# A mixture of experts computed by sorted blocks of 256 rows instead of all tokens, in a two-layer state-space kernel

## The chip, the cores and the metric

One Trainium2 chip, one NeuronCore. The metric is the device time of one execution in microseconds (us); the lower the better. The core has a matrix engine (PE), a vector engine (DVE), a scalar engine (ACT), GpSimd (POOL) and a sync engine (SP) whose only work here is to issue DMAs. [...] engines wait for each other by semaphores.

## The reference

Four images of 384 channels and 32 x 32 positions (1024 tokens each), all in fp32, pass two layers. Each layer adds a "mixing" branch and then a feed-forward branch.

- Layer 0 mixing: four selective scans per image (rows, columns, and both reversed), then a layernorm. Layer 0 feed-forward: a small factored one.
- Layer 1 mixing: a Mamba block with 768 inner channels (input projection, a convolution of four taps, selective scan, gate, output projection, layernorm).
- Layer 1 feed-forward: a mixture of four experts. Gate scores are softmaxed, the two largest of four are kept and rescaled to sum 1, and each expert is a 384 -> 1536 -> 384 network with GELU. The result for a token is the sum of its two experts' outputs, weighted by the gates.

The parts that matter:

```python
dt = softplus(dt @ dt_proj_w.T + dt_proj_b)
# for t in tokens:
dA    = exp(dt_t * A)
h_new = dA * h_prev + dt_t * B_t * x_t        # 16 states per channel
y_t   = sum(h_new * C_t)
# experts, for each token:
out = sum over the two chosen e of gate_e * (gelu(x @ w1[e] + b1[e]) @ w2[e] + b2[e])
```

## The kernel before, in words

**Units and passes.** The work is cut in half-images of 512 tokens, called units `(b, h)`: image `b`, half `h`. The selective scans of both layers make 48 passes of three parts, and each part has four steps, so there are 576 steps in all. A step handles 32 channels times 16 states as four 128 x 512 tiles.

**One step.** POOL multiplies `dt*u` by B (`times_b`, line 1184, one instruction of 128 x 2048). ACT makes four decays `exp(dt*A)` in PSUM (`decay`, line 1190). DVE scans four times (`scan`, line 1199). The product with C is shared: DVE does two to four of the quarters (`times_c`, line 1230), POOL the rest (`times_c_pool`, line 1241). PE adds the states up with four small matmuls (`add`, line 1219) into the PSUM bank `acc`. The products of four consecutive steps lie in a ring of four tiles `s`.

**The order.** No scheduler works at run time. The kernel's Python contains a planner (`Plan`). It holds a cost for each instruction, keeps a planned clock for each engine, and emits instructions in the order in which that plan would start them. The step's instructions are "main" streams. Everything else (layernorms, projections, convolutions, the experts) runs as "lanes" that are fitted into the gaps, by rank. The experts have the lowest rank, so during the scans they only fill PE's gaps. When the last step is over, a job called `tail` hands the scan's buffers and its five PSUM banks to the other lanes.

**dt.** For each pass, `prep_pass` (lines 453 to 459) makes dt of three tiles: three small matmuls, bias by ACT, one `Softplus` on 128 x 1536 with its activation table loaded before it and the exp/ln table loaded again after it, then three products by POOL.

**Experts.** `front` (line 835 on) loads a finished unit of layer 1 from DRAM, normalizes it into `tb`, and works out the gates `sc`, which are zero for the two experts not chosen. `experts` runs all four experts on all 512 tokens of the unit: `first` multiplies by w1 (line 971, three matmuls of 512 columns for each of 12 hidden tiles), ACT adds the bias (line 974), `gelus` applies GELU with a table load on both sides (line 989), `second` multiplies by w2 (line 1026). `add_up` multiplies the result by the gate on DVE (lines 1055 and 1057) and adds it up on POOL (line 1060). Weights stream from DRAM in tiles of 192 KB (lines 925 and 932), 96 of them for a unit. Nearly all are issued from ACT's queue, in pieces of 512 bytes.

Of the kernel before, what the change touches and what calls it, by code (L numbers as in the profile page):

```python
# [10 lines left out]
F32 = mybir.dt.float32  # L11
AF = mybir.ActivationFunctionType
# [5 lines left out]
P = 128  # L18
# [15 lines left out]
NE = 4  # L34
QROW = 32
# [4 lines left out]
for _name, _w in (  # L40
    ("dtb0", 4 * NC),
    ("dtb1", NI),
    ("ds0", 4 * NC),
    ("d1", NI),
    ("lnw0", NC),
    ("lnb0", NC),
    ("lng1", NC),
    ("lnb1", NC),
    ("convw", NI * 4),
    ("convb", NI),  # L50
    ("kron1", NC),
    ("b1", NE * NF),
    ("b2", NE * NC),
):
    _PV[_name] = (_n, _w)
    _n += _w
# [192 lines left out]
def layers(ctx, tc, ins, out, const):  # L249
# [41 lines left out]
    tmp = Free(tiles(5, [P, NC, T], "tmp"))  # L291
# [3 lines left out]
    tbs = Free(tiles(1, [P, NC, T], "tb"))  # L295
    yas = Free(tiles(1, [P, NC, T], "ya"))
    mw1 = Free(tiles(3, [P, NC, P], "mwa"))
    mw2 = Free(tiles(3, [P, NC, P], "mwb"))
    NK = T // P
    scs = tiles(2, [P, NK, NE], "sc")  # L300
# [52 lines left out]
    x2 = {(b, h): dram.tile([D, T], F32, name=f"x2_{b}_{h}") for b in range(NB) for h in range(NT)}  # L353
    zs = {(b, h): dram.tile([DI, T], F32, name=f"z_{b}_{h}") for b in range(NB) for h in range(NT)}
# [74 lines left out]
    def prep_pass(v, p, of_u):  # L429
# [22 lines left out]
        yield ACT, 1.45 + SWITCH  # L452
        nc.scalar.activation(dt, dt, AF.Softplus)  # L453
        exp_set()
# [383 lines left out]

    units = [(b, h) for b in range(NB) for h in range(NT)]
    NQ = NF // NC  # L840
# [4 lines left out]

    def front(u):


        def gen():
            n = units.index(u)  # L850
            yield from till(lambda: n < 2 or ("gates", units[n - 2]) in plan.end)
            tb = yield from tbs.take()
            st["tb", u] = tb
            sc = st["sc", u] = scs[n % 2]
# [5 lines left out]
            for j in range(NK):  # L860
# [9 lines left out]
            red, rank, more, same = (  # L870
                scratch[:, :NK],
                scratch[:, 16:32].rearrange("p (j e) -> p j e", e=NE),
                scratch[:, 64:128].rearrange("p (j e f) -> p j e f", e=NE, f=NE),
                scratch[:, 128:192].rearrange("p (j e f) -> p j e f", e=NE, f=NE),
            )
# [31 lines left out]
            nc.vector.tensor_tensor(sc, sc, each(red), ALU.mult)  # L907
            t1.give(scratch)

        return gen  # L910

    def experts():
        made, ready, sums, w1q, w2q = [], [], [], [], []
        held = {"hid": 0}


        want1 = [(e, f) for _ in units for e in range(NE) for f in range(NF)]
        want2 = [(e, q, m) for _ in units for e in range(NE) for q0 in range(0, NQ, 2) for m in range(NC) for q in (q0, q0 + 1)]
        idle = []

        def load1(w, engine):
            if want1:
                e, f = want1.pop(0)
                of = ins["w1"][e].rearrange("(c p) f -> p c f", p=P)
                engine.dma_start(out=w, in_=of[:, :, f * P : (f + 1) * P])
                w1q.append((plan.now + LOAD + 0.7, w))

        def load2(w, engine):
            if want2:
                e, q, m = want2.pop(0)  # L930
                of = ins["w2"][e].rearrange("(q f p) d -> q p f d", p=P, f=NC)
                engine.dma_start(out=w, in_=of[q, :, :, m * P : (m + 1) * P])
                w2q.append((plan.now + LOAD + 0.7, w))

        def starts():

            while want1 or want2:
                yield from till(lambda: mw1.tiles or mw2.tiles or idle and plan.now - idle[0][1] > 8.0)
                for of, load in ((mw1, load1), (mw2, load2)):
                    if of.tiles:  # L940
                        w = yield from of.take()
                        yield SP, 0.1
                        load(w, nc.sync)
                if idle and plan.now - idle[0][1] > 8.0:
                    yield ACT, 0.1
                    if idle:
                        load2(idle.pop(0)[2], nc.scalar)

        def bank():

            yield from till(lambda: ("tail",) in plan.end or len(ps.tiles) > 1)
            return (yield from ps.take())

        def first():
            for u in units:
                yield from till(lambda: ("front", u) in plan.end)
                tb = st["tb", u]
                for e in range(NE):
                    for q in range(NQ):
                        yield from till(lambda: ("tail",) in plan.end or held["hid"] < 3 and len(tmp.tiles) > 1)  # L960
                        held["hid"] += 1
                        hid = yield from tmp.take()
                        for j in range(NC):
                            f = q * NC + j
                            yield from till(lambda: w1q)
                            t, w = w1q.pop(0)
                            yield "at", t
                            ph = yield from bank()
                            yield PE, 2.75
                            for c in range(NC):  # L970
                                nc.tensor.matmul(ph, lhsT=w[:, c, :], rhs=tb[:, c, :], start=c == 0, stop=c == NC - 1)  # L971
                            at = plan.count
                            t = yield ACT, 0.75
                            nc.scalar.activation(hid[:, j, :], ph, AF.Identity, bias=pv("b1", e * NF + f, 1))  # L974

                            load1(w, nc.scalar)
                            while idle and idle[0][0] < at:
                                load2(idle.pop(0)[2], nc.scalar)
                            ps.give(ph)
                        made.append((t, hid))  # L980
                tbs.give(tb)

        def gelus():
            for _ in range(len(units) * NE * NQ):
                yield from till(lambda: made)
                t, hid = made.pop(0)
                yield "at", t
                t = yield ACT, 1.45 + SWITCH
                nc.scalar.activation(hid, hid, AF.Gelu)
                exp_set()  # L990
                ready.append((t, hid))

        def second():
            for u in units:
                yield from till(lambda: ("front", u) in plan.end)
                sc = st["sc", u]
                ya = yield from yas.take()
                yield SP, LOAD
                nc.sync.dma_start(out=ya, in_=x2[u].rearrange("(c p) t -> p c t", p=P))
                for e in range(NE):  # L1000

                    gate = yield from t1.take()
                    yield ACT, 1.6
                    for j in range(NK):
                        nc.scalar.activation(gate[:, j * P : (j + 1) * P], ident, AF.Copy, scale=sc[:, j, e : e + 1])
                    if e == NE - 1:
                        plan.end["gates", u] = plan.now
                    pgb = yield from ps.take()
                    yield PE, 0.95
                    nc.tensor.matmul(pgb, lhsT=ones, rhs=gate, start=True, stop=True)  # L1010
                    yield ACT, 0.65
                    nc.scalar.copy(gate, pgb)
                    ps.give(pgb)
                    for q in range(0, NQ, 2):
                        yield from till(lambda: len(ready) > 1)
                        pair = [ready.pop(0) for _ in range(2)]
                        yield "at", pair[1][0]
                        for m in range(NC):
                            py = yield from bank()
                            for k in range(2):  # L1020
                                yield from till(lambda: w2q)
                                t, w = w2q.pop(0)
                                yield "at", t
                                t = yield PE, 2.75
                                for j in range(NC):
                                    nc.tensor.matmul(  # L1026
                                        py,
                                        lhsT=w[:, j, :],
                                        rhs=pair[k][1][:, j, :],
# [16 lines left out]
        def add_up():  # L1046
            for _ in range(len(units) * NE * NQ // 2 * NC):
# [13 lines left out]
                t1.give(yt)  # L1061
                held["sum"] = False

        return [starts, first, gelus, second, add_up]

# [407 lines left out]
```

## Time and profile before

| | |
|---|---|
| median of three runs | 5608.84 us (5605.87 to 5609.27) |
| the profiled execution, time | 5604.8 us |
| the profiled execution, span | 5602.7 us |
| PE busy | 4604.9 us, 82% |
| DVE busy | 4200.0 us, 75% |
| POOL busy | 4101.4 us, 73% |
| ACT busy | 3345.2 us, 60% |
| DMA | 746.27 MB, mean 133 GB/s |
| matmuls of w1 and w2 (lines 971, 1026) | 2304 of 512 columns |

The span runs from the first to the last instruction. The profile records each fp32 matmul as two, so 2304 matmuls are 4608 records. The execution has two stretches. Up to about 4448 us the scans run; the last `add` starts at 4447.23 us. After that only PE is busy, with the experts of the last units. The 40-slice rows of the page show both at a glance: each digit is the busy share of one slice of 140 us, in tenths.

### The profile page before, as it was taken

What the parts mean: (1) busy time and instruction counts of PE and PEld (TensorE: products, weight loads), DVE (VectorE), ACT (ScalarE), POOL (GpSimd) and SP (SyncE); (2) the same over time, 40 slices, a digit from 0 to 9 for tenths busy, and PEclk for the clock granted to TensorE, in tenths of its full rate; (3) what the DMA queues carried; (4) which work ended last, traced back from release to release, by engine and by line L of the source; (5) the groups of instructions that cost most, each with busy time, mean ns of one, the idle gap of its engine ahead of it and who ended that gap; (6) DMA issues with size and microseconds to landing.
All of it is one profiled execution on the core that took longest, in us unless ns stands there. A gap on an engine that the chain in (4) does not pass through costs nothing. (4 is left out here: it accounts for less than half of the span.)

```text
span 5602.7 us, 43582 instructions
## 1 busy us (share of the span) xinstructions
PE 4604.9 (82%) x12448; PEld 1582.0 (28%) x12448; DVE 4200.0 (75%) x5718; ACT 3345.2 (60%) x4611; POOL 4101.4 (73%) x1559
## 2 busy tenths in 40 slices
PE   4545577856888889888888888888987999999999
PEld 1000112211222223332223222222332344444444
DVE  4999998999999998999899998989778710101000
ACT  3444477755566777866666776767666544444442
POOL 4999998999899998998898988988788711011111
PEclk7666778867899998998899899988999999999999
DMA  3433333444454344544454545444445422222221
GB/s 117 136 129 112 125 125 120 161 135 155 160 172 165 123 155 151 172 159 139 145 169 154 173 145 159 149 149 140 138 162 162 138 90 75 88 80 79 76 85 59
DMA packets 598833, 746.27 MB, mean 133 GB/s; under 512 B 67232, under 2 KB 419648, under 8 KB 580160
## 3 DMA queue, kind: packets, MB, share of 16 engines
q1 hardware_dynamic: 247968, 428.97, 23.5%
q10 hardware_dynamic: 350624, 314.51, 17.7%
q8 instruction: 100, 1.64, 0.1%
q14 instruction: 141, 1.16, 0.1%
HBM read 633.65 MB, written 109.67 MB: 133 GB/s over the span
## 5 line engine op out<-in xcount | busy, mean ns | idle before, releaser
L1184 POOL TENSOR_TENSOR s<-dtus,bt 128x2048 f32<-128x2048 f32 x576 | 2607.5, 4534 | 122.9 <-PE acc L1219 62.7
L1190 ACT ACTIVATE da<-dts,a 128x512 f32<-128x512 f32 x2304 | 1505.6, 682 | 1025.9 <-DVE s L1230 851.1
L1219 PE MATMUL acc<-s,four 128*32 128x512 f32 x4608 | 1068.6, 708 | 595.9 <-POOL s L1241 365.3
L1241 POOL TENSOR_TENSOR s<-s,ct 128x1024 f32<-128x1024 f32 (+1 forms) x497 | 978.6, 1970 | 216.3 <-DVE s L1199 71.6
L1230 DVE TENSOR_TENSOR s<-da,ct 128x512 f32<-128x512 f32 x1489 | 960.3, 679 | 0.3
L1199 DVE TENSOR_TENSOR_SCAN da<-da,state,s 128x512 f32<-128x512 f32 x740 | 916.0, 1275 | 25.8 <-POOL s L1184 13.4
L1199 DVE TENSOR_TENSOR_SCAN da<-da,s 128x512 f32<-128x512 f32 x749 | 885.5, 1217 | 53.4 <-POOL s L1184 35.8
L1026 PE MATMUL ps<-tmp,mwb 128*128 128x512 f32 x1152 | 571.2, 639 | 37.9 <-DMA mwb<-in_w_dram 35.3
L971 PE MATMUL ps<-tb,mwa 128*128 128x512 f32 x1176 | 578.2, 633 | 8.8 <-ACT tmp L450 4.7
L1060 POOL TENSOR_TENSOR ya<-ya,t 128x512 f32<-128x512 f32 x144 | 183.2, 1272 | 543.0 <-DVE t L1057 295.0
L1219 PEld LDWEIGHTS acc<-s,four 128*32 128x32 f32 x4608 | 157.4, 115 | 1388.5 <-POOL s L1241 592.5
L1199 DVE TENSOR_TENSOR_SCAN s<-da,state,s 128x512 f32<-128x512 f32 x412 | 510.0, 1268 | 4.1 <-ACT da L1190 4.0
L1199 DVE TENSOR_TENSOR_SCAN s<-da,s 128x512 f32<-128x512 f32 x403 | 473.2, 1204 | 6.4 <-ACT da L1190 6.2
L1060 POOL TENSOR_TENSOR dtus<-dtus,t 128x512 f32<-128x512 f32 x48 | 60.7, 1265 | 483.4 <-DVE t L1055 266.5
L1026 PEld LDWEIGHTS ps<-tmp,mwb 128*128 128x128 f32 x1152 | 225.0, 203 | 383.5 <-issue 309.4
L971 PEld LDWEIGHTS ps<-tb,mwa 128*128 128x128 f32 x1176 | 224.9, 200 | 364.1 <-issue 287.1
L270 ACT ACT_TABLE_LOAD x249 | 319.5, 1283 | 5.0 <-PEq L1464 0.7
L670 PE MATMUL ps<-big,w 128*128 128x512 f32 x576 | 286.7, 642 | 36.7 <-DMA w<-in_w_in_dram 22.8
L974 ACT ACTIVATE tmp<-ps,pvt 128x512 f32<-128x512 f32 x224 | 151.8, 678 | 202.9 <-PE ps L971 197.3
L459 POOL TENSOR_TENSOR tmp<-tmp,big 128x256 f32<-128x256 f32 (+1 forms) x192 | 199.9, 1063 | 74.8 <-ACT tmp L453 74.7
L1055 DVE SCALAR_TENSOR_TENSOR t<-da,pvt,t 128x512 f32<-128x512 f32 x29 | 21.8, 751 | 293.9 <-PE da L1026 293.9
L441 PE MATMUL ps<-xd,dtw 12*128 12x512 f32 (+1 forms) x288 | 184.8, 739 | 39.8 <-DMA dtw<-in_w_dt_dram 23.5
(235 smaller groups left out, 5387.8 us busy)
## 6 DMA issues: line engine op xcount, KB each, us to landing
dts<-dts ACTq DMA_DIRECT2D x288, 512.0 KB
dtus<-dts SPq DMA_DIRECT2D x144, 1024.0 KB
dts<-tmp SPq DMA_DIRECT2D x384, 192.0 KB
mwa<-in_w_dram ACTq DMA_DIRECT2D x265, 192.0 KB
mwb<-in_w_dram ACTq DMA_DIRECT2D x261, 192.0 KB
bt<-rows SPq DMA_DIRECT2D x192, 256.0 KB
ct<-rows SPq DMA_DIRECT2D x192, 256.0 KB
ct<-in_w_dram ACTq DMA_DIRECT2D x116, 192.0 KB
```

Source lines behind the costliest of these rows:

```text
L270: nc.scalar.preload_act_table_set("natural_log_exp_and_others")
L459: nc.gpsimd.tensor_tensor(to, by, u[:, c], ALU.mult)
L670: nc.tensor.matmul(pi, lhsT=w[:, c, :], rhs=u[:, c], start=c == 0, stop=c == NC - 1)
L971: nc.tensor.matmul(ph, lhsT=w[:, c, :], rhs=tb[:, c, :], start=c == 0, stop=c == NC - 1)
L1026: nc.tensor.matmul(py, lhsT=w[:, j, :], rhs=pair[k][1][:, j, :], start=k + j == 0, stop=k * NC + j == 2 * NC - 1,)
L1060: nc.gpsimd.tensor_tensor(ya[:, m, :], ya[:, m, :], yt, ALU.add)
L1184: nc.gpsimd.tensor_tensor(ss[i % NSR], dtus[part_of(i) % 2], rep(bts[i % 4], NG), ALU.mult)
L1190: nc.scalar.activation(das[x], dts[(2 * part_of(i) + x // 2) % 3][:, x % 2, :], AF.Exp, scale=v["a"][:, g, m : m + 1])
L1199: nc.vector.tensor_tensor_scan(d if in_psum else s, d, s, 0.0 if v["first"] else state[:, v["slot"], j, x : x + 1], ALU.mult, ALU.add)
L1219: nc.tensor.matmul(acc[x * QP : (x + 1) * QP, :], lhsT=four, rhs=ss[i % NSR][:, x, :], start=m == 0, stop=m == 3)
L1230: nc.vector.tensor_tensor(ss[i % NSR][:, x, :], das[x], cts[i % 4], ALU.mult)
L1241: nc.gpsimd.tensor_tensor(s[:, m:, :], s[:, m:, :], rep(cts[i % 4], NG - m), ALU.mult)
```

## The change

The experts no longer see all tokens. The change has these parts:

- **Routing** (`front`, longer by about 60 lines). From the ranks of the gates it counts, by matmuls with a triangular matrix and with ones, the place of each token in the list of each chosen expert. Each expert has 1024 places for an image. The normalized rows are transposed by PE, copied by ACT and written to their places in a DRAM buffer `slot_x` by indirect DMAs issued by POOL: two for each 128 tokens.
- **A table** (`blocks`). For each image 11 blocks of 256 places are listed, whatever the tokens chose; a table holds each block's first place and its expert.
- **Block work** (`experts`). For each of 44 blocks SP reads the place and the expert from the table into registers. It loads 256 rows, the bias and the weights by addresses from these registers. PE transposes the rows; w1 is applied with 256 columns, w2 with 384 columns and the tokens as output rows. The result goes to a DRAM buffer `slot_y`. Weights are now laid out so that one load is 384 KB in pieces of 3072 bytes, and all are issued from SP's queue.
- **Combining** (`combine`). For each 128 tokens two indirect DMAs fetch the two results. PE multiplies them by diagonal matrices of the gates, adds the bias rows in the same PSUM tile, and DVE adds the sum to the residual.
- **Zeroing** (`zero`). All of `slot_x` and `slot_y` are filled with zeros once, by 48 DMAs of 768 KB.
- **dt** in `prep_pass`: `Softplus` and its table loads are replaced by `Abs`, `Exp`, `Ln` (all in the loaded table) and one DVE instruction, `max(x, 0) + ln(1 + exp(-|x|))`.
- **Buffers**: six instead of five `tmp` tiles; the tiles `tb`, `ya` and six weight tiles of 192 KB go, four of 384 KB come; GELU is applied to a whole block at once in the scans and in two halves in the tail.

The core of the diff:

```diff
+BLK = 256
+SLOTS = L
+NBLK = (2 * L + NE * (BLK - 1)) // BLK
 ...
-    tmp = Free(tiles(5, [P, NC, T], "tmp"))
+    tmp = Free(tiles(6, [P, NC, T], "tmp"))
 ...
-    mw1 = Free(tiles(3, [P, NC, P], "mwa"))
-    mw2 = Free(tiles(3, [P, NC, P], "mwb"))
+    mws = Free(tiles(4, [P, 2 * D], "mw"))
 ...
-        yield ACT, 1.45 + SWITCH
-        nc.scalar.activation(dt, dt, AF.Softplus)
-        exp_set()
+        for func, of, more in ((AF.Abs, dt, {}), (AF.Exp, dtu, {"scale": -1.0}), (AF.Ln, dtu, {"bias": 1.0})):
+            yield ACT, 1.45
+            nc.scalar.activation(dtu, of, func, **more)
+        yield DVE, 1.85
+        nc.vector.scalar_tensor_tensor(dt, dt, 0.0, dtu, ALU.max, ALU.add)
 ...
+    def zero():
+        z = yield from t1.take()
+        nc.vector.memset(z[:, :D], 0.0)
+        n = NE * SLOTS // P // 8
+        for slot in (*slot_x, *slot_y):
+            for x in range(8):
+                to = slot.rearrange("(n p) d -> p n d", p=P)[:, n * x : n * (x + 1), :]
+                yield SP, 12.0
+                nc.sync.dma_start(out=to, in_=rep(z[:, :D], n))
+        t1.give(z)
 ...
+                for k in range(2):
+                    t = 3.0 + (yield POOL, 1.3, max(t, sent))
+                    nc.gpsimd.indirect_dma_start(
+                        out=slot_x[b % 2],
+                        out_offset=bass.IndirectOffsetOnAxis(ap=slot[:, k, j : j + 1], axis=0),
+                        in_=row[:, :D],
+                        in_offset=None,
+                    )
 ...
+        def weights():
+            for b, i in every:
+                yield from known(b)
+                yield SP, 1.0
+                e = nc.sync.value_load(tables[b][:, 1, i : i + 1], min_val=0, max_val=NE - 1)
+                of = ins["w12"][bass.DynSlice(e, 1)].rearrange("o q p m -> (o q) p m")
+                for q in range(2 * NQ):
+                    w = yield from mws.take()
+                    yield SP, 0.1
+                    nc.sync.dma_start(out=w, in_=of[q])
+                    wq.append((plan.now + LOAD + 2.0, w))
 ...
+                for q in range(NQ):
 ...
+                    for k in range(2):
+                        for c in range(NC):
+                            nc.tensor.matmul(
+                                ph[:, k * BLK : (k + 1) * BLK],
+                                lhsT=w[:, c, k * P : (k + 1) * P],
+                                rhs=turned[:, c],
+                                start=c == 0,
+                                stop=c == NC - 1,
+                            )
 ...
+                    for f in range(2):
+                        for k in range(2):
+                            nc.tensor.matmul(
+                                py[k][:, :D],
+                                lhsT=by_f(hids[half_])[:, at_ + f, k * P : (k + 1) * P],
+                                rhs=w[:, f],
+                                start=2 * q + f == 0,
+                                stop=2 * q + f == NF - 1,
+                            )
 ...
+                for k in range(2):
+                    t = yield POOL, 1.3
+                    nc.gpsimd.indirect_dma_start(
+                        out=y[k],
+                        out_offset=None,
+                        in_=slot_y[b],
+                        in_offset=bass.IndirectOffsetOnAxis(ap=slots[u][:, k, j : j + 1], axis=0),
+                    )
```

The lines `second`, `add_up` and the old weight lanes are removed.

## The prediction

> **What bounds the kernel now.** I read the page's forty slices first, to see which engine is full when.
>
> ```profile
> span 5602.7 us, 43582 instructions
> ...
> PE   4545577856888889888888888888987999999999
> ...
> DVE  4999998999999998999899998989778710101000
> ...
> POOL 4999998999899998998898988988788711011111
> ```
>
> In the first 31 slices or so DVE and POOL are full and PE is not; in the last eight PE alone is full. So there are two stretches with different limits, and a busy share over the span says little. The windows give the second stretch numbers (busy us and records of PE and PEld, DVE, ACT, POOL; then clock, DMA share, GB/s):
>
> ```profile
> 4480.00:4760.00 280.00, 279.99 (x662) 124.70 (x661) 30.46 (x60) 128.41 (x145) 30.35 (x24) 0.99 0.28 82
> 4760.00:5040.00 280.00, 277.51 (x661) 123.75 (x660) 25.80 (x45) 121.10 (x134) 31.59 (x25) 0.99 0.28 82
> ```
>
> PE is busy 280 of 280 us at clock 0.99, DMA is at 28%. Anything that shortens PE's work there shortens the kernel by as much. Next the timeline, for what one matmul costs:
>
> ```profile
> 4551.85 2.74 PE L862 MATMUL da<-wgate,tb 128*128 128x4 f32 x24
> ...
> 5002.44 2.74 PE L971 MATMUL da<-tb,bt 128*128 128x512 f32 x6
> 5002.44 0.19 PEld L971 LDWEIGHTS da<-tb,bt 128*128 128x128 f32 x1 [0.24 <-issue]
> ...
> 5002.87 0.19 PEld L971 LDWEIGHTS da<-tb,bt 128*128 128x128 f32 x1 [0.24 <-issue]
> ...
> 5003.30 0.19 PEld L971 LDWEIGHTS da<-tb,bt 128*128 128x128 f32 x1 [0.24 <-issue]
> ```
>
> Records follow each other every 0.429 us (5002.44, 5002.87, 5003.30) at 512 columns: 0.838 ns a column, weight loads beside it. With 4 columns, 24 records take 2.74 us, some 0.11 us each: that is the floor of a load and its matmul. From these the tail can be added up. Counted in the built order, after the last `add` stand 1301 matmuls of 512 columns (1236 of the experts) and 48 small: 2602 x 0.429 + 96 x 0.11 = 1127 us. Measured from the last `add` (ends 4448) to the last matmul (ends 5596): 1148. PE idles 2% there; 6 us of stores follow.
>
> In the first stretch the experts are only fillers. What they cost there is seen on DVE, by group (busy, mean ns, idle before it):
>
> ```profile
> L1055 DVE SCALAR_TENSOR_TENSOR t<-ps,pvt,t 128x512 f32<-128x512 f32 x45 | 33.3, 739 | 14.6 <-PE ps L1026 14.6
> ...
> L1057 DVE TENSOR_TENSOR t<-ps,t 128x512 f32<-128x512 f32 x42 | 28.5, 679 | 58.1 <-PE ps L1026 58.1
> ...
> L1060 POOL TENSOR_TENSOR ya<-ya,t 128x512 f32<-128x512 f32 x87 | 111.2, 1278 | 38.9 <-DVE t L1057 30.9 <-DVE t L1055 7.7 <-ACT da L1190 0.2
> ```
>
> DVE works 62 us for them and stands still 73 us behind late matmuls; POOL works 111 us.
>
> **The change part by part: the tail.** In the built order 22 of 44 blocks have had their w1 by the last `add`, and the tail holds 792 matmuls of 256 columns (w1), 532 of 384 (w2), 375 of 128 (transposes, combining), 36 of 512 and 58 tiny. At two records each and 0.838 ns a column: 792 x 2 x 0.2145 = 340; 532 x 2 x 0.322 = 342; 375 x 2 x 0.107 = 80; 31; 13. Sum 806 us instead of 1127.
>
> [...] The trace: 0.19 us LDWEIGHTS inside every 0.429 us record, at no cost. [...] With the load exposed at the 0.11 us floor, the tail's 3398 records of 128 to 384 columns would cost 374 us more and the whole gain would be gone. The trace decides: 0.19 also fits into 0.2145. I take no extra cost[...].
>
> Beside PE's 806 us: ACT per block, by its rows, 12 biases of 256 columns (between 389 ns at 128 and 682 at 512, so 0.49), 2 GELUs x 1.48, 4 table loads x 1.28, four copies: some 17 us beside PE's 31 (36 x 2 x 0.2145 + 24 x 2 x 0.322 = 30.9). Hidden. Loads: 12 x 393 KB of weights plus rows in and out, 5.5 MB a block, 178 GB/s. Before, 82 GB/s took a 0.28 share, so a full share would be 293: 178 is 0.6 of it. Hidden, with seven weight tiles (18 us) ahead, but no slice of the page shows over 173.
>
> The ends of the tail. At its start the third image isn't routed: the last scatter, its landing, a load of rows and transposes stand before its first block, while PE has some 35 us of projections, layernorms and combining, which wait for POOL themselves. I take 12 us idle (5 to 35). At its end a chain is new: two ACT copies (1), store (4), 16 gathers on POOL one after the other (16 x 1.2 = 19), landing, nine matmuls, DVE and the store of the output (10): 34 us, of which 17 are PE work counted above. PE's other idling I put at 25 (before 21). Tail: 806 + 25 + 12 + 17 = 860 against 1154, a gain of 294.
>
> **The scans.** DVE, by counts in the built order up to the last scan: 48 new `max + ln` of 1536 columns, by 739 ns at 512 and 1.05 ns a further column (1754 against 679 ns) 1.81 us each: +87. Lines 1055 and 1057: -62. Products with C 1489 to 1438, x 0.679: -35. Two layernorms more, 2 x 4.9, and some 150 small instructions for gates, places and tables at 0.2 (line 897: 205 ns): +41. Combining (8) and 32 memsets: +6. Sum +37. Idle: -73 behind lines 1055 and 1057. The new instruction waits for `Ln`; line 392, which waits for ACT likewise, idles 0.8 us each, so +38; behind it queue the scans. POOL: line 1060 -111; products with C, 360 x 2.361 + 146 x 1.275 against 976: +60; 60 indirect DMAs.
>
> What one of these costs no row shows. Below: a plain DMA issue takes 0.37 us on the queues (line 925). [...] DVE is over 90% busy in the scans, but with scans and two-operand products; its copies are of one column (line 1213, 0.15 us). I take 1.2 [...]: +72, POOL +21. [...] Each scatter also waits on POOL for the one before it to land, but one or two POOL instructions (4.53 us, line 1184) stand between.
>
> ACT loses 48 x 2 table loads for softplus (123 us) and 74 for GELU (95), gains two instructions a pass, 96 x 1.48 (142), and about 10 of small work: some -65. It is off the path; its decays wait for DVE.
>
> SP's queue: 250 weight loads move from ACT's queue to SP's, with 65 register loads, 42 row transfers, 22 bias loads and 48 zeroings (37.7 MB, 2.7 us each at the 293 GB/s above). They stand among loads that already wait there for POOL:
>
> ```profile
> SPq L481 <- POOL s L1184: 972.0, 86, 29.3
> SPq L1181 <- POOL s L1184: 833.6, 135, 37.2
> ```
>
> The cover is that a step's operands are double- or fourfold buffered, about four steps (30 us) ahead. If it is gone, a late weight holds PE, `add` stands behind it, and the ring of four `s` stops POOL. I put lateness at +15.
>
> DVE: 37 - 73 + 38 + 15, nearly +20; POOL +21 fits. Scans 4448 + 20 = 4468 (-70 to +100). Span 4468 + 860 = 5328; with the 2.1 us that lie around the span before (5604.8 - 5602.7), 5330. The median of the runs is 4 us above the profiled execution, so I forecast 5334.
>
> **The rivals.**
> 1. *The scans get longer* by a dearer indirect DMA or late loads, while the tail gains as computed. [...] For: DVE and POOL are full already, and new work is put on both. Against: the counts nearly cancel.
> 2. *The tail becomes bound by loads.* At 150 GB/s, near the scans' mean, a block takes 5.5 MB / 150 = 36.7 us, 22 x 5.8 = 128 more: 5462. Against: the low share of 0.28, and longer pieces now.
> 3. *Slower: weights behind waiting loads in SP's queue.* 250 loads now stand behind the waits above, whose mean is 11 us (972 / 86). The gain to be eaten is 275 us: it decides from 1.1 us of unhidden lateness for each of the 250. With 2 us each, +500 - 275: 5834. For: in-order SP couples POOL, weights and PE. Against: PE has more slack in the scans, since its fillers shrink from 1068 x 0.858 = 916 us to 677.
> 4. *The cut is not what it says:* the exposed weight load above, 5334 + 374 = 5708, also slower; from 0.08 us a record (275 / 3398). The number of rows itself can't fail: 44 blocks are fixed, 0.6875 of before.
>
> **How the numbers follow.** The tail's gain with scans near par (5250 to 5430, likeliest 5334): 0.75. Rival 1: 0.12, rival 2: 0.07; both faster. Rivals 3 and 4: 0.05 together. A chance of 0.01 remains for no change; a measurement can tell 0.2%, 11 us. Faster 0.94, same 0.01, slower 0.05. The range 5245 to 5480 takes in most of rivals 1 and 2 and leaves out under 0.2.
>
> **What would show it.** Right: the last `add` between 4380 and 4550; then PE at 9 in every slice but the last; w1 records 0.21 us apart; no line 1055 or 1057 and no wait in their place on DVE over 1 us each; POOL's indirect DMAs near 1 us. Wrong: PE idle behind DMA `mw` for tens of us (rivals 2, 3); DVE waits for ACT before `max + ln` of several us; w1 records 0.3 us apart; scatters that stop POOL before line 1184's successor.

## The result, and the profile after

The changed kernel takes 5573.17 us (median of five runs, 5570.28 to 5584.16) against 5608.26 us for the kernel before (five runs beside it, 5600.78 to 5609.27). The ratio is 0.9945, 95% interval 0.993 to 0.9959: a gain of 35 us, where 275 us were forecast. The direction was right, and the size was far off.

The page of the profiled execution after (its time 5573.17 us, span 5571.4 us), rows of forty slices of 139 us:

```profile
span 5571.4 us, 49082 instructions
...
PE   4555567866466888888878877887898787999998
...
DVE  5999998999989999999989899999964995100000
...
POOL 3999998999887999989888879998854795101001
```

DVE stands at 4 tenths or more up to the 34th slice, where it was the 32nd before, and the stretch that belongs to PE alone has become shorter. So the scans grew and the tail shrank. Measured from the trace with the end of the last scan on DVE as the border: scans 4444.7 -> 4662.5 us (+218), tail 1158.0 -> 908.9 us (-249). Three windows of the new tail, the last one up to its end (busy us and records of PE and PEld, DVE, ACT, POOL; then clock, DMA share, GB/s):

```profile
4760.00:5040.00 280.00, 273.85 (x1095) 199.56 (x1094) 11.93 (x48) 130.84 (x199) 13.41 (x14) 0.99 0.55 177
5040.00:5320.00 280.00, 270.51 (x1110) 197.53 (x1109) 4.43 (x8) 114.44 (x186) 15.21 (x16) 0.99 0.55 175
5320.00:5571.00 251.00, 228.53 (x859) 166.34 (x857) 4.43 (x8) 91.31 (x147) 15.16 (x16) 0.87 0.44 139
```

In the first two windows PE is busy 97 to 98% of the time, and loads take a 0.55 share at 175 to 177 GB/s, close to the 0.6 and 178 GB/s of the forecast. Up to its last stretch the tail did what was said of it; the last window, with a mean clock of 0.87, is taken up below. The scans did not, and the groups of DVE show the first reason. The first line is the new `max + ln`. The second is a layernorm's subtraction of the same shape, 128 x 1536 (before: line 374, mean 1748 ns), with one operand in PSUM:

```profile
L479 DVE SCALAR_TENSOR_TENSOR tmp<-tmp,tmp 128x1536 f32<-128x1536 f32 x48 | 150.4, 3134 | 56.2 <-ACT tmp L477 56.0
...
L396 DVE TENSOR_TENSOR big<-big,ps 128x1536 f32<-128x1536 f32 x24 | 41.9, 1747 | 60.0 <-PE ps L394 60.0
```

Line 479 was priced at 1.81 us and has a mean of 3.134. Its answer by source gives 1732/2641/6862 ns as least, median and largest: same instruction, same shape. The timeline of DVE and POOL shows what the longest one does (start, duration in us):

```profile
3846.79 1.29 POOL L1460 TENSOR_TENSOR s<-s,ct 128x512 f32<-128x512 f32 x1
3847.31 6.86 DVE L479 SCALAR_TENSOR_TENSOR tmp<-tmp,tmp 128x1536 f32<-128x1536 f32 x1
3848.02 4.54 POOL L1403 TENSOR_TENSOR s<-dtus,bt 128x2048 f32<-128x2048 f32 x1
3854.10 1.22 DVE L1418 TENSOR_TENSOR_SCAN da<-da,s 128x512 f32<-128x512 f32 x1
```

It starts while POOL is inside a product with C. It lasts through the rest of that and through the whole of `times_b` after it (which ends at 3852.56), and then needs 1.6 us more, about its own time. POOL's `times_b` takes its usual 4.54 us: here only DVE pays. The same is seen on the small instructions of the routing, here in the table of blocks:

```profile
3288.14 0.96 POOL L1244 DMA_INDIRECT tmp<-ys,slot  x1 [0.30 <-issue]
3288.38 0.15 DVE L1028 TENSOR_TENSOR t<-next,nums 128x4 f32<-128x4 f32 x1
3288.57 5.11 DVE L1029 TENSOR_TENSOR t<-t,nums 128x16 f32<-128x16 f32 x1
3289.12 4.51 POOL L1403 TENSOR_TENSOR s<-dtus,bt 128x2048 f32<-128x2048 f32 x1
3293.71 0.17 DVE L1030 TENSOR_REDUCE t<-t 128x4 f32<-128x16 f32 x1
```

A comparison of 16 columns, 0.18 us elsewhere, starts while POOL is still in an indirect DMA. It takes 5.11 us and ends as POOL's next instruction ends. Nothing in the column of waits tells this: a stalled instruction counts as busy.

The second reason lies near the end of the scans. Pass 43 (from its first `times_b` to that of pass 44) takes 212 us, against 150 before. It has a hole, in which POOL and DVE stand still (two waits: who waits, for what, us). It ends with the third line, in which the step waits for the load of `dt*u`, the last link of image 3's chain from layer 0 to layer 1:

```profile
DVE tmp L479 <- ACT tmp L477: 52.2, 1, 52.2
...
POOL tmp L484 <- DVE tmp L479: 108.4, 1, 108.4
...
4254.74 4.51 POOL L1403 TENSOR_TENSOR s<-dtus,bt 128x2048 f32<-128x2048 f32 x1 [15.45 <-DMA dtus<-dts]
```

Indirect DMAs on POOL are not a reason (the groups of scatter and gather):

```profile
L1008 POOL DMA_INDIRECT xs<-t,slot x54 | 55.9, 1035 | 85.0 <-ACT t L1004 57.4 <-DMA xs<-t,slot 19.6 <-issue 4.4
L1244 POOL DMA_INDIRECT tmp<-ys,slot x34 | 32.6, 958 | 383.4 <-DMA ys<-dtus 359.6 <-issue 7.2 <-DMA z<-tmp 6.8
```

### The profile page after: what moved, and what is told of

Read it like the earlier page. It is cut to its first block, busy times and chain, and to the rows that moved or that the text cites. A ratio compares the mean times of both kernels' runs of the same rounds, so it can differ in the third digit from the quotient of the medians.

```text
span 5571.4 us, 49082 instructions
## 1 busy us (share of the span) xinstructions
PE 4291.8 (77%) x14104; PEld 1882.3 (34%) x14104; DVE 4274.1 (77%) x5740; ACT 3150.3 (57%) x4735; POOL 4073.2 (73%) x1504
## 5 line engine op out<-in xcount | busy, mean ns | idle before, releaser
L1403 POOL TENSOR_TENSOR s<-dtus,bt 128x2048 f32<-128x2048 f32 x576 | 2616.5, 4550 | 123.9 <-PE acc L1438 66.2
L1438 PE MATMUL acc<-s,four 128*32 128x512 f32 x4608 | 1165.2, 751 | 707.8 <-POOL s L1460 445.8
L1460 POOL TENSOR_TENSOR s<-s,ct 128x1024 f32<-128x1024 f32 (+1 forms) x506 | 1049.6, 2076 | 261.4 <-DVE s L1418 106.5
L1449 DVE TENSOR_TENSOR s<-da,ct 128x512 f32<-128x512 f32 x1438 | 924.9, 679 | 0.3
L1418 DVE TENSOR_TENSOR_SCAN da<-da,state,s 128x512 f32<-128x512 f32 x706 | 872.0, 1273 | 27.9 <-ACT da L1409 25.8
L1418 DVE TENSOR_TENSOR_SCAN s<-da,state,s 128x512 f32<-128x512 f32 x446 | 550.3, 1266 | 3.6 <-ACT da L1409 3.5
L1135 PE MATMUL ps<-tmp,mw 128*128 128x256 f32 x1740 | 424.5, 398 | 10.4 <-ACT tmp L1177 3.5
L1154 PE MATMUL ps<-mw,tmp 128*128 128x384 f32 x1140 | 417.1, 513 | 12.3 <-ACT tmp L1199 11.6
L1135 PEld LDWEIGHTS ps<-tmp,mw 128*128 128x128 f32 x1740 | 336.0, 198 | 142.1 <-ACT da L1409 21.6
L1154 PEld LDWEIGHTS ps<-mw,tmp 128*128 128x128 f32 x1140 | 219.4, 199 | 227.1 <-issue 63.7
L477 ACT ACTIVATE tmp<-tmp 128x1536 f32<-128x1536 f32 x144 | 212.2, 1474 | 2.8 <-ACT da L1409 1.8
```

Source lines behind the costliest of these rows:

```text
L477: nc.scalar.activation(dtu, of, func, **more)
L1135: nc.tensor.matmul(ph[:, k * BLK : (k + 1) * BLK], lhsT=w[:, c, k * P : (k + 1) * P], rhs=turned[:, c], start=c == 0, stop=c == NC - 1,)
L1154: nc.tensor.matmul(py[k][:, :D], lhsT=by_f(hids[half_])[:, at_ + f, k * P : (k + 1) * P], rhs=w[:, f], start=2 * q + f == 0, stop=2 * q + ...
L1403: nc.gpsimd.tensor_tensor(ss[i % NSR], dtus[part_of(i) % 2], rep(bts[i % 4], NG), ALU.mult)
L1418: nc.vector.tensor_tensor_scan(d if in_psum else s, d, s, 0.0 if v["first"] else state[:, v["slot"], j, x : x + 1], ALU.mult, ALU.add)
L1438: nc.tensor.matmul(acc[x * QP : (x + 1) * QP, :], lhsT=four, rhs=ss[i % NSR][:, x, :], start=m == 0, stop=m == 3)
```

## The experiments

Theory A: DVE's new instructions read both operands from SBUF and stall behind POOL; this lengthens the scans. Theory B: the chain of image 3 before pass 44 starves of tiles that the experts' blocks hold. Rivals: the loads, the zeroing, the indirect DMAs or the order itself lengthen the scans. In the table, scans end with the last scan on DVE, and the tail is the rest of the span; differences are in us. The passes' lengths are taken from the starts of `times_b`. Scans, tail and passes are those of the profiled execution, and the median is over all runs of a kernel. An edit that changes a planned cost also changes the order that the planner writes. In e_one_operand alone the order is the changed kernel's; what a new order does by itself was not tested.

| kernel | median us | ratio to before, 95% interval | scans end | tail | pass 43 |
|---|---|---|---|---|---|
| before | 5608.3 | | 4444.7 | 1158.0 | 150 |
| changed | 5573.2 | 0.9945 (0.993 to 0.9959) | 4662.5 | 908.9 | 212 |
| b_abs | 5686.6 | 1.0142 (1.0127 to 1.0158) | 4586.5 | 1101.4 | 169 |
| b_ln1p | 5499.0 | 0.9805 (0.9792 to 0.9819) | 4397.4 | 1101.1 | 98 |
| e_one_operand | 5526.1 | 0.986 (0.9845 to 0.9875) | 4607.8 | 906.5 | 212 |
| e_ln_psum | 5507.4 | 0.9823 (0.9809 to 0.9836) | 4576.2 | 929.1 | 201 |
| e_ln1p | 5440.0 | 0.9701 (0.9687 to 0.9714) | 4508.2 | 932.3 | 153 |
| e_route_psum | 5597.2 | 0.9981 (0.997 to 0.9993) | 4623.8 | 966.2 | 212 |
| v1 | 5414.6 | 0.9659 (0.9646 to 0.9672) | 4456.8 | 949.3 | 154 |
| v2 | 5426.1 | 0.9676 (0.9663 to 0.9689) | 4452.4 | 955.3 | 146 |
| v5 | 5430.7 | 0.9689 (0.9675 to 0.9702) | 4416.1 | 1000.8 | 96 |
| e_holdx41 | 5608.2 | 1.0007 (0.9999 to 1.0015) | 4580.0 | 1021.9 | 104 |
| e_hold | 5710.3 | 1.0184 (1.017 to 1.0198) | 4568.6 | 1143.8 | 91 |

**b_abs: the dt part alone, in the kernel before.**

```diff
-        yield ACT, 1.45 + SWITCH
-        nc.scalar.activation(dt, dt, AF.Softplus)
-        exp_set()
+        for func, of, more in ((AF.Abs, dt, {}), (AF.Exp, dtu, {"scale": -1.0}), (AF.Ln, dtu, {"bias": 1.0})):
+            yield ACT, 1.45
+            nc.scalar.activation(dtu, of, func, **more)
+        yield DVE, 1.85
+        nc.vector.scalar_tensor_tensor(dt, dt, 0.0, dtu, ALU.max, ALU.add)
```

> The kernel before with one part of the change alone: softplus becomes Abs, Exp, Ln on ScalarE and one max-and-add on VectorE; the experts stay as they were. Theory A (the max-and-add, with both operands in SBUF, is stretched while GpSimd is inside an instruction): slower than before by 60 to 150 us, its 48 records with a mean near 3 us and some over 5 us, and nearly all of the loss in the scans. Rival (the scans were lengthened by the rows' indirect DMAs, the zeroing and the dearer loads, the new dt costing only its own 1.8 us x 48, less the table loads): within 40 us of before, mean of the max-and-add at most 2 us.

Measured: 5686.6 us, 79 us slower than before. The group of the new instruction in this kernel:

```profile
L456 DVE SCALAR_TENSOR_TENSOR tmp<-tmp,tmp 128x1536 f32<-128x1536 f32 x48 | 158.4, 3300 | 12.7 <-ACT tmp L454 12.7
```

The stall needs none of the experts' part. This also answers the rival on the zeroing. Its DMAs are issued between 353 and 967 us, within passes 3 to 10. These take 687 us before, 696 in b_abs and 702 in the changed kernel; with the cheaper dt of two runs below they take 679 (b_ln1p) and 688 (e_ln1p). So zeroing, with all else that is new there, costs 5 to 9 us. The scans grew by 142 us and the tail shrank by 57. The shorter tail is not the longer scans' doing: b_ln1p has the same tail with scans 189 us shorter. Both leave fewer expert matmuls to the tail (1170 and 1176, before 1236).

**e_one_operand: the same place, one operand.**

```diff
-        nc.vector.scalar_tensor_tensor(dt, dt, 0.0, dtu, ALU.max, ALU.add)
+        nc.vector.tensor_scalar(dt, dtu, 0.0, None, ALU.max)
```

> The changed kernel with the max-and-add replaced by a max with a constant that reads one SBUF operand of the same shape and type at the same place; the values of dt leave out the part max(x, 0). Theory A (two SBUF operands are what makes VectorE wait for GpSimd): the mean falls from 3.13 us to under 2 us, no record above 3 us, the single wait of 52 us behind it may stay; time 40 to 100 us less. Rival (VectorE waits for something else that ends there, a semaphore or the bandwidth of SBUF): mean stays near 3 us, records of 5 to 7 us remain, time within 20 us.

Measured: 5526.1 us, 47 us less. The time fits theory A, but its records do not:

```profile
L479 DVE TENSOR_SCALAR tmp<-tmp 128x1536 f32<-128x1536 f32 x48 | 111.5, 2322 | 59.1 <-ACT tmp L477 59.0
```

The mean is 2.322 us and the largest 5.76; 16 records exceed 3 us, where none was expected. The eight records that met no POOL instruction, or one for 0.1 us only, took 0.95 us, the others 2.60 on average. So two operands are not the condition, and theory A as I had put it fell. At 0.95 us this instruction runs nearly twice as fast as the 1.75 us of the other. What the stretched records seen so far share is that they read SBUF alone. In the changed kernel none of the 2304 scans (line 1418, 1.16 to 1.31 us) and of DVE's 1438 products with C (line 1449, 0.66 to 0.71 us) is stretched, and each of them reads one operand from PSUM. Theory A2 is that an operand in PSUM is what spares an instruction the wait for POOL, and the next run tests it.

**e_ln_psum: same arithmetic, one operand in PSUM.**

```diff
-        for func, of, more in ((AF.Abs, dt, {}), (AF.Exp, dtu, {"scale": -1.0}), (AF.Ln, dtu, {"bias": 1.0})):
+        for func, of, more in ((AF.Abs, dt, {}), (AF.Exp, dtu, {"scale": -1.0})):
 ...
-        yield DVE, 1.85
-        nc.vector.scalar_tensor_tensor(dt, dt, 0.0, dtu, ALU.max, ALU.add)
+        for c in range(NC):
+            pl = yield from ps.take(True)
+            yield ACT, 0.65
+            nc.scalar.activation(pl, dtu[:, c, :], AF.Ln, bias=1.0)
+            yield DVE, 0.75
+            nc.vector.scalar_tensor_tensor(dt[:, c, :], dt[:, c, :], 0.0, pl, ALU.max, ALU.add)
+            ps.give(pl)
```

> The changed kernel, same arithmetic of dt, but Ln writes into a PSUM bank per 512 columns and the max-and-add (now three of 128x512) reads one operand from SBUF and one from PSUM. Theory A2 [...]: 144 records of 0.7 to 0.8 us, none above 1 us, busy time about 107 us in place of 150, time 20 to 70 us less than the changed kernel. Rival (any such operation at this place is stretched): records of several us remain, busy time 150 us or more, time within 15 us or slower by the three bank turns.

Measured: 5507.4 us, 66 us less than the changed kernel. First the group, then a stretch of the timeline:

```profile
L483 DVE SCALAR_TENSOR_TENSOR tmp<-tmp,ps 128x512 f32<-128x512 f32 x144 | 97.2, 676 | 43.1 <-ACT ps L481 42.5 <-DMA mw<-in_w_dram 0.6
```

```profile
4407.80 2.34 POOL L1465 TENSOR_TENSOR s<-s,ct 128x1024 f32<-128x1024 f32 x1
4408.44 0.67 DVE L483 SCALAR_TENSOR_TENSOR tmp<-tmp,ps 128x512 f32<-128x512 f32 x1
4409.03 1.28 DVE L1423 TENSOR_TENSOR_SCAN da<-da,state,s 128x512 f32<-128x512 f32 x1
```

No record exceeds 0.71 us, although 98 of the 144 lie wholly inside a POOL instruction, as this one does. The same operation on the same values, moved from two SBUF operands to one in SBUF and one in PSUM, is no longer stretched behind POOL. This bears out theory A2 at this place, and the scans and the products with C, with one operand in PSUM throughout, fit it.

**e_ln1p and b_ln1p: dt without a DVE instruction.** ln(1 + exp(x)), in the changed kernel and in the one before.

```diff
-            nc.scalar.activation(dt[:, c, :], pd, AF.Identity, bias=bias)
+            nc.scalar.activation(dt[:, c, :], pd, AF.Exp, bias=bias)
 ...
+        yield ACT, 1.45
+        nc.scalar.activation(dt, dt, AF.Ln, bias=1.0)
```

> The changed kernel with dt as ln(1 + exp(x)): the Identity that takes x out of PSUM becomes Exp, one Ln with bias 1 follows, and the Abs, the second Exp and the max-and-add on VectorE go. Theory A: the 150 us of max-and-add and the waits behind it go, the scans end 100 to 190 us earlier, time 90 to 180 us less (about 5400 to 5480). Rival (loads, zeroing and indirect DMAs lengthened the scans): only the max-and-add's own 48 x 1.8 us can go and part of that is not on the path, time 20 to 60 us less.

> The kernel before with dt as ln(1 + exp(x)) alone, no operation on VectorE added, the experts as they were: it splits the change into its two parts in a form in which dt costs VectorE nothing. Theory A2 (dt's VectorE operation, not the end of softplus, is what cost time): same as before or up to 40 us less (the table loads around softplus go), so that the experts' part alone is worth the difference to the 5440 us of the changed kernel with this dt, some 130 to 170 us. Rival (any change of dt's form delays the passes): slower than before by 20 us or more.

Measured: e_ln1p 5440.0 us, 133 us less than the changed kernel; its scans end 154 us earlier, and 23 us come back in the tail. b_ln1p takes 5499.0 us, 107 us less than before, where at most 40 were expected. So leaving softplus and its table loads was worth far more than I thought. It did not come in even shares: pass 43 is 52 us shorter and the tail 57, while the other passes together are 4 us longer. Whether ACT's freed time or the planner's new order did this was not separated. The form that the change chose for dt cost b_abs - b_ln1p = 188 us against this one. The two runs also split the change: with this dt the experts' part is worth 5499 - 5440 = 59 us (scans +111, tail -169), where 130 to 170 were expected. The changed kernel with softplus kept was not run.

**e_route_psum, and v1: the routing's scratch in PSUM.** Each of the small DVE instructions gets at most one operand in SBUF; v1 has this and ln(1 + exp(x)) together.

```diff
-            scratch = yield from t1.take()
+            scratch = yield from ps.take()
+            in_sbuf = yield from t1.take()
 ...
-            nc.vector.tensor_tensor(same, same, ahead.unsqueeze(1).to_broadcast(shape), ALU.mult)
-            nc.vector.tensor_tensor(more, more, same, ALU.add)
+            nc.vector.tensor_tensor(same2, same, ahead.unsqueeze(1).to_broadcast(shape), ALU.mult)
+            nc.vector.tensor_tensor(more, more, same2, ALU.add)
 ...
```

> The changed kernel with the scratch of the routing and of the table of blocks held in a PSUM bank, arranged so that each small VectorE operation has at most one operand in SBUF (three more small operations a unit). Theory A2: the routing's records fall from a mean of 0.445 us in the scans to 0.25 us or less, with hardly one above 1 us, which is 40 to 55 us of VectorE; time 10 to 50 us less than the changed kernel. Rival (the small operations' stalls are covered by other waits, or the held bank costs as much): the records shorten but the time stays within 10 us; or they don't shorten.

> dt as ln(1 + exp(x)) and the routing's scratch in PSUM together, in the changed kernel. Theory A2: the two add up, 10 to 40 us below the 5440 us of the run with ln(1 + exp(x)) alone, near 5400 to 5430 us. Rival (one wait takes the place of the other): within 10 us of 5440 us.

Measured: in the changed kernel 204 routing records lie in the scans and take 92.6 us, 19 of them above 1 us. In e_route_psum 177 lie there and take 39.4 us, one above 1 us. The scans end 39 us earlier. Yet the time is 5597.2 us, 24 us more, a miss, as the tail is 57 us longer. About 0.6 blocks fewer are done by the end of the scans (counted by w1 and w2 matmuls, 19 us at 31 us each). The rest lies at the tail's start; one line of PE's waits and one window show it:

```profile
PE ps L1111 <- DMA s<-xs: 12.1, 1, 12.1
...
4674.00:4724.00 50.00, 35.90 (x109) 22.59 (x108) 11.04 (x11) 17.13 (x38) 17.40 (x18) 0.68 0.48 170
```

The scans end earlier, but the third image's routing does not come earlier: its table is ready at 4631 us (4634 in the changed kernel). That is 8 us after the scans' end, where it was 29 us before it. So its first rows are loaded 59 us after the scans' end and not 26, and PE stands still for them for 12.1 us. Between 4685 and 4753 us the clock is 0.5 for 61 us, and records of 512 columns follow each other every 840 ns there, not every 429; the first 140 us of the changed kernel's tail have 24 us at 0.5. My estimate from these is 19 (blocks) + 12 (PE's idling) + 19 (clock) = 50 of the 57 us. Together with the cheaper dt the same edit helps: v1 takes 5414.6 us, 25 us less than e_ln1p, with no routing record above 1 us; scans 51 us shorter, tail 17 longer. Its page:

```profile
span 5406.1 us, 49002 instructions
...
PE   4545568865567889879798877878888779999998
...
DVE  4999999999899999999998899989958891000000
```

v1 is the fastest kernel of this study and beats both: 0.9659 of before. Its scans end at 4456.8 us, 12 us later than before.

**e_hold and e_holdx41: blocks held back before pass 44**, in the changed kernel; e_hold holds rows and hidden tiles from pass 36, e_holdx41 only new rows, from pass 41.

```diff
+        def late():
+            return ("pass", 36) in plan.end and ("pre", 1, NB - 1, 0) not in plan.end
 ...
-                yield from till(lambda: held["x"] < 3 if tailing() else held["x"] < 2 and len(tmp.tiles) > 2)
+                yield from till(lambda: held["x"] < 3 if tailing() else held["x"] < 2 and len(tmp.tiles) > 2 and not late())
 ...
-                yield from till(lambda: tailing() or len(tmp.tiles) > 2)
+                yield from till(lambda: tailing() or len(tmp.tiles) > 2 and not late())
```

(The last pair is in e_hold alone; e_holdx41 has 41 for 36.)

> The changed kernel, the experts' blocks being started neither by their rows nor by their hidden tiles between the end of preparing pass 36 and the end of the preparation of image 3's second layer (first half). Theory B (the chain of image 3 between its two layers starves of tiles and PSUM banks that the blocks hold): pass 43 shrinks from 212 us to 130 to 160 us, scans end 50 to 110 us earlier, one or two blocks move into the tail at about 20 us each, time 30 to 90 us less. Rival (the chain is limited by its own work or its loads): pass 43 stays within 20 us of 212, the tail gets the moved blocks, time the same to 40 us more.

> The changed kernel, no further block's rows being fetched between the end of preparing pass 41 and the end of the preparation of image 3's second layer (first half); a block already fetched goes on. Theory B2 (the blocks' tiles and banks open the hole before pass 44, but each block kept out comes back in the tail at about 30 us): pass 43 falls from 212 us to under 170 us, scans end 40 to 100 us earlier, the tail grows by 30 to 110 us, time within 30 us of the changed kernel. Rival (the hole is a pure loss): 40 to 100 us less than the changed kernel.

Measured: pass 43 falls from 212 to 91 and 104 us, so in the changed kernel the blocks do open the hole. The scans end 94 and 83 us earlier, as expected. But e_hold is 137 us slower and e_holdx41 35 us slower than the changed kernel. The tails grow by 235 and 113 us, for 8.0 and 3.6 blocks fewer done in the scans: 29 and 31 us a block. The first expectation had the mechanism and left out the price: it counted one or two moved blocks where eight moved. The second had the price too; its time and tail lie 5 and 3 us outside what was expected.

**v2 and v5: the hole in v1.** v2 holds as above from pass 42. v5 holds nothing back, but serves the chains' requests for `tmp` tiles first.

```diff
-            sq = yield from tmp.take()
+            sq = yield from tmp.take(True)
```

(and likewise the chains' other requests for `tmp` tiles).

> As the run before it (dt as ln(1 + exp(x)), routing in PSUM), and the experts' blocks started neither by rows nor by hidden tiles between the end of preparing pass 42 and that of the preparation of image 3's second layer (first half): a shorter hold than the one that cost 137 us. Theory B2 (a hold trades the hole before pass 44 against expert blocks at about 30 us each in the tail): scans end 20 to 60 us earlier, one or two blocks (30 to 60 us) move into the tail, time within 20 us of the run before it. Rival (the hole is a pure loss): 40 to 60 us less than the run before it.

> dt as ln(1 + exp(x)), the routing's scratch in PSUM, and the tile requests of the chains between the layers (layer norm, the feed-forward, the second layer's preparation and its end) served ahead of those of the experts' blocks; nothing is held back by time. It asks whether SBUF tiles open the hole before pass 44. Theory B2 (tiles do, and a block delayed is a block in the tail): pass 43 falls from 154 us to 130 us or less, scans end 20 to 60 us earlier, the tail grows by about as much, time within 25 us of the 5415 us without it. Rival (PSUM banks or the chain's own work): pass 43 stays near 154 us and the time too. Rival 2 (the order was simply bad): 25 to 60 us less than without it.

Measured: v2 leaves pass 43 at 146 us, so it did not test what it was made for; its time (5426.1) cannot be told from v1's, as the intervals overlap. v5 closes the hole (96 us; passes 33 to 35 and 40 to 42 become 22 and 30 us longer), scans end 41 us earlier, the tail grows by 52, and the time is 5430.7, 16 us above v1. The order in which SBUF tiles are given out is thus enough to close the hole, and closing it gains nothing: what the scans win, the tail loses.

## Why the prediction was right and wrong

- **The tail: right in its work, 49 us short in size.** Forecast 860 against 1154 (gain 294), measured 908.9 against 1158.0 (gain 249); 21.8 of 44 blocks had been done before it, forecast 22. The mis-sized term is the chain at the end, put at 34 us. From the last w2 matmul (ends at 5503.9 us) to the end it took 67.5 us. In the last 51 us the granted clock is 0.50, and combining's records of 128 columns stand 214 ns apart, where those between 5131 and 5506 us, at a clock of 1.00, take 112 ns. The sum had priced them at full clock; before, the last 100 us of the tail had a clock of 0.98.
- **Weight loads: right.** Rival 4, the exposed load, did not occur: 1110 records fit into 280 us, and PE's weight loads (197.5 us) lie beside its 270.5 us of matmuls.
- **The scans: wrong.** Forecast +20, measured +218. The failed step is the price of the new DVE instructions. "48 new `max + ln` ... 1.81 us each: +87" was read off rows with one operand in PSUM; measured 150.4 us, as both operands lie in SBUF (97.2 us with one in PSUM, e_ln_psum). "some 150 small instructions ... at 0.2" was read off line 897, a group without a long record; measured 92.6 us for 204 in the scans. The dt stall alone, with the same arithmetic kept on DVE, is worth 86 us of scans and 66 us of time (e_ln_psum). Without any DVE instruction for dt it is 154 us of scans (e_ln1p, which also drops two ACT instructions a pass), and 51 us more with the routing in PSUM (v1): 206 of the 218. This includes 58 us of pass 43, which falls to 154 us in v1. The other 12 us are a balance: 59 us more in v1's scans than in b_ln1p's, less the 47 us by which b_ln1p's are shorter than before's.
- **The risk was looked for at the wrong instruction.** The prediction sought it in the indirect DMAs, on POOL's side, and took 1.2 us each, its author's estimate. They took 0.96 to 1.04 us. The price fell due on DVE's side: 150.4 us on line 479, where 87 had been put down.
- **"ACT ... is off the path": wrong in the other direction, it seems.** b_ln1p gains 107 us by the end of softplus and its table loads, if not by the order that came with it. The sum had given this nothing; the change's dt spent that gain and 79 us more.
- **Waits for `Ln`, +38 at 0.8 each:** in their place six waits of 56 us, of which one has 52.2; it lies in the hole of pass 43. **Lateness, +15:** weights were not late. What the sum had no term for is that hole, by which pass 43 grew 62 us.
- **Rivals.** Rival 1 had the right sign and the wrong cause. Rivals 2 and 3 did not occur: PE's waits for a weight DMA are 1.3 us in w1's line and none in w2's.
- **Where the expected gain went.** With dt at its cheapest and the routing unstalled (v1), the experts' part is worth 5499 - 5415 = 84 us, not 275: the scans are 59 us longer than b_ln1p's, 56 of it in pass 43 (the other passes' differences cancel), and the tail is 152 shorter. Of the tail's missing gain, 57 us had already gone in b_ln1p. v1's own tail is 89 us longer than the forecast: 23.5 blocks are left to it and not 22 (some 46 us at 31 us each), and from 5341 us to its end it too runs at a clock of 0.5, for 65 us. That v1's scans end at 4457 us, near the forecast 4468, is luck in part: what dropping softplus takes from the scans (47 us in b_ln1p) was not in the sum.

## What to carry to other kernels

Price an instruction by a row with the same kinds of operands, not only the same shape: on VectorE a second operand in SBUF, or a one-operand form like that of e_one_operand, cost up to the length of two GpSimd instructions here (6.86 us where the least was 1.73, and 5.76 where it was 0.95). Look for the spread within a group (least, median, largest), since a stall behind another engine counts as busy and shows in no wait (5.11 us for a comparison that takes 0.18 elsewhere). And when a filler fills the gaps of another stage, count both stages: a hole closed by taking the filler away came back in the tail at 29 to 31 us a block.

## What the hardware showed unexpectedly

- A 16-column DVE instruction with two SBUF operands took 5.11 us when it met the end of an indirect DMA on POOL and an instruction of 4.51 us right behind it. One of 1536 columns took 6.86 us through two POOL instructions in a row: having waited through the first did not put it ahead of the second. Of 48 such records, 4 waited like this in the changed kernel, 3 in b_abs and 5 in e_one_operand. POOL's own durations stayed the same (4550 ns mean, 4534 before).
- The hint was in the trace of before, and small: a `tensor_scalar` of 4 columns (line 905) had a mean of 664 ns over eight records, where the shortest took 0.17 us. A subtraction with two SBUF operands (line 886) took 0.62 to 1.01 us in the scans and 0.18 us in the tail, where POOL is mostly idle.
- Taking away one pair of table loads for each pass (1.28 us each, 48 pairs) with dt's softplus went with a gain of 107 us, though ACT was only 60% busy. None of it lies in the ordinary passes: 52 us are in pass 43 and 57 in the tail.
